# A graph layer on one TensorE: program order in the passes, and key fetches for two steps at once

## The chip, the cores and the metric

The kernel runs on one core of a Trainium2 chip. The metric is the device time of one execution in microseconds. The kernel before takes 17037.5 us, the median of three runs (17037.39 to 17084.01).

## What is computed

A node's features are normalised and cut off at zero. Every edge gives a message from its destination node and the difference of its source node to it, and each node adds the mean of its messages:

```python
h = jnp.maximum(_layernorm(x, axis=-1), 0.0)

local = h[dst]
nbr = h[src]
y = einsum('ec,oc->eo', concat([local, nbr - local]), W) + b
s = segment_sum(y, dst)
cnt = segment_sum(ones, dst)[:, None]
x = x + where(cnt > 0, s / maximum(cnt, 1.0), 0.0)
```

There are 100,000 nodes of 64 features and 3,300,000 edges, sorted by destination; the sources are random. Since the message is linear, what costs time is the sum, for each node, of the rows `h[src]`. The rows are held as three bf16 parts and a one, 193 columns (`CE`).

## The kernel before

The sum is computed in two ways that run side by side.

**Windows and passes.** The first 256 windows of 7936 edges are sorted by source (`sort_windows`, on VectorE (DVE) and ScalarE (ACT)) and the sorted keys written to `ksort` in DRAM. DVE then counts for each window where each block of source rows begins (line 596, `pos` at line 605) and makes a table `at` of addresses for the key fetches. A *cell* is one window's keys in 256 source rows; a *step* handles two cells (`i`), of 32 slots each, for the four windows (`QW`) of a set. `fill_slots` fetches the keys of a step, for all sets at once, by four indirect transfers of 128x32 keys (`kf`, line 716), issued by GpSimd (POOL), turns them into the numbers `srs` and `dts` and stores these. Keys beyond 32 in a cell are the *spill*: `find_beyond` fetches them by 128 indirect transfers of one key a row (`kx`, line 692), and DVE turns them into rows `xs` (line 698).

A pass keeps 40 blocks of `h` rows as tables (`tab`, line 759, fetched by SyncE (SP)) and goes through 64 sets of four windows, 40 steps each. In a step, `pick` multiplies one-hots `gh` (line 808) with the tables by 4 matmuls of 128x128 (line 829), ACT copies the result to `gs` (line 831), and `put` adds it by 16 quarter matmuls with one-hots `dh` (line 331 by `one_hot`, matmuls at line 838) into `total`. The loop goes by pairs of steps, with 8 matmuls of picks and 32 of puts each; picks run ahead of puts by two steps. After a set DVE reduces `total` to `wsums`. There are 5 passes: pass 0, in whose course the keys of later steps are fetched and the spill is found; passes 1 to 3 in a loop on the chip (line 957); pass 4 in two halves (line 959), in which sums are added to `acc` (line 880) and each set's spill is multiplied in (`rows_x`, line 794).

**Chunks.** The other 1,268,384 edges are 354 chunks of 128x28 edges (`chunks`). POOL gathers the rows of `h` by 28 indirect transfers a chunk (`nb`, line 388), DVE makes one-hots `hot` (line 331), TensorE (PE) sums them into `ps` by 28 matmuls (line 399), DVE reduces them to `sums` (lines 404 and 406), and POOL adds these to `acc` (line 357 by an indirect transfer, with addresses `to` from line 352, or line 362). There are six buffers of seven gathers for `nb`, so POOL may be 42 gathers ahead; the code of a matmul is emitted 21 gathers behind. 90 chunks belong to the sort stage and pass 0, 66 (`KB`) to each of passes 1 to 3, 33 to each half of pass 4. While windows are sorted and pass 0 runs, `gathers` interleaves them by estimated times (`GATHER` 1270 ns a gather); in `turn` they are spread evenly over the pairs of steps.

**Order.** The order of instructions on each engine is set by a scheduler, except where `last[engine]` ties one instruction behind another (`behind`, `tc.issue_after`). Nothing ties a chunk's matmuls or the picks and puts on PE, so the scheduler places them. Additions are put off: `add_later((LAG - 1) * J, ...)` (line 408) makes a chunk's addition due 56 gathers after its sums.

## Time and profile before

| what | value |
|---|---|
| median of three runs | 17037.5 us |
| the profiled execution | 17007.46 us |
| its span, from first to last instruction | 17005.8 us |
| TensorE matmuls busy | 12381.4 us (73% of the span) |
| DVE busy | 12270.0 us (72%) |
| POOL busy | 12313.7 us (72%) |
| ACT busy | 7284.1 us (43%) |
| 9912 gathers of chunks on POOL (line 388) | 10098.9 us busy, 3811.3 us idle ahead of them |

Busy shares are means over stages with different limits, so the table alone doesn't tell what bounds the kernel. A row of instructions by line has the line, the engine, the operation, what is written and read, the count, then busy time and mean nanoseconds of one, and the idle time of the engine just ahead with what ended it; "issue" there means that the engine waited for nothing that the profile shows. A row of waits has the waiting instruction, what released it, the sum in us, the count and the longest. A row of a line's instructions has the least, median and largest duration in ns, then the first begin and the last end in us.

### The profile page before, as it was taken

To read this page: it belongs to the slowest core of one execution; us is meant where nothing else is said; L and a number is where in the kernel's file an instruction comes from. 1 tells how busy PE (TensorE), PEld (TensorE's weight loads), DVE (VectorE), ACT (ScalarE), POOL (GpSimd) and SP (SyncE) were. 2 spreads that over 40 slices of the span, in tenths; PEclk is the share of its full clock that TensorE was granted. 3 is DMA by queue.
4 is the path that set the end of the run, shared out by engine and by line. 5 is a ranking of instruction groups with operands and counts; after the bars stand their busy time and mean duration, and the time that the engine had idled before them with its cause. 6 is when DMAs were issued, how large, how long until landed. Compare 5 with 4: busy or idle time off the path is not lost. (4 is left out here: it accounts for less than half of the span.)

```text
span 17005.8 us, 639895 instructions
## 1 busy us (share of the span) xinstructions
PE 12381.4 (73%) x266812; PEld 9784.7 (58%) x266812; DVE 12270.0 (72%) x31051; ACT 7284.1 (43%) x15555; POOL 12313.7 (72%) x11723
## 2 busy tenths in 40 slices
PE   6111111559999799999699999699999698858775
PEld 5011000447777577777577777477777576647664
DVE  6999982558878687777587777587777576647663
ACT  5244480335555344444354444254444343324331
POOL 4777777665675477777677777767777778767885
PEclk7555555779999899999799999799999798879887
DMA  7322222324454455555455555455555565556556
GB/s 293 70 39 40 49 49 58 86 73 115 120 121 120 112 128 123 124 124 122 112 127 123 124 124 123 110 128 124 122 124 123 112 125 112 113 100 121 112 111 250
DMA packets 1672971, 1949.85 MB, mean 115 GB/s; under 512 B 1065318, under 2 KB 1078766, under 8 KB 1665070
## 3 DMA queue, kind: packets, MB, share of 16 engines
q1 hardware_dynamic: 1194800, 1341.60, 27.4%
q0 software_dynamic: 471200, 541.36, 20.4%
q8 instruction: 2090, 34.24, 0.8%
q10 hardware_dynamic: 4032, 25.69, 0.4%
q14 instruction: 849, 6.96, 0.1%
HBM read 1652.22 MB, written 255.28 MB: 112 GB/s over the span
## 5 line engine op out<-in xcount | busy, mean ns | idle before, releaser
L388 POOL DMA_INDIRECT nb<-h,si x9912 | 10098.9, 1019 | 3811.3 <-issue 2714.6
L831 ACT CAST gs<-gp 128x386 bf16<-128x386 f32 x12800 | 5591.9, 485 | 7358.8 <-PE gp L829 6820.4
L331 DVE TENSOR_TENSOR dh<-dt,upto 128x512 bf16<-128x512 int16 x12800 | 4575.9, 419 | 1979.7 <-PE total L838 1697.2
L838 PE MATMUL total<-gs,dh 32*128 32x193 bf16 x200704 | 5542.2, 251 | 304.8 <-DVE dh L331 288.3
L829 PE MATMUL gp<-tab,gh 128*128 128x193 bf16 x50176 | 5509.6, 253 | 129.8 <-ACT gs L831 83.6
L838 PEld LDWEIGHTS <-dh 32*128 32x128 bf16 x200704 | 4125.9, 96 | 1490.7 <-issue 1099.5
L829 PEld LDWEIGHTS <-gh 128*128 128x128 bf16 x51200 | 4404.5, 100 | 1000.1 <-issue 861.6
L399 PE MATMUL ps<-nb,hot 128*128 128x193 bf16 x9912 | 2106.6, 278 | 3659.3 <-DMA nb<-h,si 2151.3
L808 DVE TENSOR_SCALAR gh<-srs,who_f 128x768 bf16<-128x768 int16 (+1 forms) x10240 | 3415.0, 393 | 643.5 <-PE gp L829 638.5
L399 PEld LDWEIGHTS <-hot 128*128 128x128 bf16 x9912 | 896.7, 105 | 4107.8 <-issue 2294.4
L331 DVE TENSOR_TENSOR hot<-near,upto 128x512 bf16<-128x512 int16 (+1 forms) x2832 | 925.6, 382 | 397.4 <-PE ps L399 393.0
L460 ACT COPY tmp<-keys 128x1536 f32<-128x1536 f32 (+26 forms) x525 | 647.7, 1244 | 1043.3 <-DVE keys L462 880.0
L716 POOL DMA_INDIRECT kf<-ksort,at x784 | 788.5, 1006 | 238.9 <-issue 228.9
L461 DVE TENSOR_TENSOR keys<-tmp,keys 128x1536 f32<-128x1536 f32 (+26 forms) x525 | 746.8, 1457 | 68.4 <-ACT tmp L460 67.2
L462 DVE TENSOR_TENSOR keys<-tmp,keys 128x1536 f32<-128x1536 f32 (+26 forms) x525 | 748.3, 1454 | 1.1
L868 DVE TENSOR_REDUCE wsums<-whole 128x512 f32<-128x1536 f32 x320 | 613.2, 1916 | 3.7 <-issue 2.1
L404 DVE TENSOR_REDUCE sums<-ps 128x64 f32<-128x192 f32 x354 | 123.6, 349 | 535.6 <-PE ps L399 532.4
L880 POOL DMA_DIRECT2D acc<-wsums x256 | 345.1, 1348 | 105.2 <-DMA acc<-wsums 91.0
L865 DVE COPY whole<-total 128x386 f32<-128x386 f32 x640 | 325.6, 550 | 52.2 <-ACT whole L863 52.2
L536 ACT ACTIVATE junk<-keys,bound 128x543 bf16<-128x543 f32 x450 | 337.4, 750 | 16.9 <-DVE keys L462 3.6
L863 ACT COPY whole<-total 128x386 f32<-128x386 f32 x640 | 276.4, 484 | 124.8 <-PE total L838 120.8
L362 POOL DMA_DIRECT2D acc<-sums x264 | 272.7, 1033 | 42.7 <-DMA acc<-wsums 17.4
(163 smaller groups left out, 4233.2 us busy)
## 6 DMA issues: line engine op xcount, KB each, us to landing
srs<-sr_d SPq DMA_DIRECT2D x2560, 320.0 KB
nb<-h,si POOLq DMA_INDIRECT x9912
part_d<-wsums SPq DMA_DIRECT2D x256, 260.0 KB
prev<-part_d SPq DMA_DIRECT2D x256, 260.0 KB
tab<-h SPq DMA_DIRECT2D x46, 970.0 KB
dt<-dt_d SPq DMA_DIRECT2D x2560, 10.0 KB
h<-parts SPq DMA_DIRECT2D x28, 1358.0 KB
dt_d<-dt SPq DMA_DIRECT2D x40, 640.0 KB
```

What stands on the lines that cost most here:

```text
L331: nc.vector.tensor_tensor(out.rearrange("p k (a d) -> p k a d", d=D), numbers[:, :, None].to_broadcast(shape), upto[:shape[0], :n].rearran ...
L388: last[POOL] = nc.gpsimd.indirect_dma_start(out=nbs[e // JN][:, e % JN], out_offset=None, in_=h3, in_offset=bass.IndirectOffsetOnAxis(ap=o ...
L399: nc.tensor.matmul(ps[:, :CE], lhsT=hots_of[d // JH][:, d % JH], rhs=nbs[d // JN][:, d % JN, :CE], start=jd == 0, stop=jd == J - 1)
L460: last[ACT] = nc.scalar.copy(tmp, lo)
L461: nc.vector.tensor_tensor(lo, tmp, hi, ALU.min)
L462: last[DVE] = nc.vector.tensor_tensor(hi, tmp, hi, ALU.max)
L716: last[POOL] = nc.gpsimd.indirect_dma_start(out=kf[:, c, r * KS:r * KS + KS], out_offset=None, in_=ksort, in_offset=bass.IndirectOffsetOnA ...
L808: nc.vector.tensor_scalar(ghots[v, k][:, part, a:z].rearrange("p c i s -> p (c i s)"), srs[v, k][:, a:z].rearrange("p c i s -> p (c i s)") ...
L829: nc.tensor.matmul(gp[:, i], lhsT=ghots[v, k][:, b, c, i], rhs=of[:, :CE], start=b == 0, stop=b == NT - 1)
L831: nc.scalar.copy(gs[t], gp)
L838: nc.tensor.matmul(total[:, r, b * CE:b * CE + CE], lhsT=dh[at, i, b * P:b * P + P], rhs=rows_of[at, i, :CE], start=begin and i == 0 and b ...
L868: nc.vector.tensor_reduce(sums[:, :, :C], whole[:, :, :C3].rearrange("p k (s c) -> p k c s", s=3), axis=AX.X, op=ALU.add)
```

## The change

1. `in_turn` ties the chunk matmuls, the first matmul of every pick and put and those of a set's own rows to the program's order on PE. `turn` starts that order afresh.
2. A chunk's addition is due 14 gathers (`JH`) after its sums instead of 56.
3. The four fetches of a step now fetch 95 keys from each address instead of 32 and serve two neighbouring cells (`kw`). The second cell's keys begin `far` behind the first; for every bit of `far` a `copy_predicated` on DVE moves the keys by that power of two. For this the two halves of a step become two contiguous ranges of source rows, so the tables are loaded by two transfers each. There are 392 such fetches and 4 plain ones instead of 784.
4. A window's spill may hold 32 keys instead of 64: 64 fetches `kx` of which four go out at a time, in order on POOL, and `xs` is computed four turns later, behind the latest `dh`. Each set has one `rows_x` fetch instead of two, and its matmuls are half as many.
5. `KB` is 64, so 98 chunks belong to the sort stage and pass 0.
6. A flag sends inputs with a cell of 64 or more keys, or more than 32 spilled keys in a window, down another way. In the inputs here the largest cell has 42 keys and a window has at most 17 spilled.

```diff
-KB = 66
+KB = 64
...
-SPILL = 2 * KS
+SPILL = KS
+NBITS = 6
+KW = KS + 2 ** NBITS - 1
...
+        def in_turn(ins):
+
+            if ins.ins.engine in last:
+                tc.add_manual_dep(ins.ins, last[ins.ins.engine].ins.name,
+                                  mybir.DependencyInfo(mybir.DependencyClass.NoSync, mybir.DependencyReason.DATA),
+                                  reason="in turn")
+            last[ins.ins.engine] = ins
...
-                    nc.tensor.matmul(ps[:, :CE], lhsT=hots_of[d // JH][:, d % JH], rhs=nbs[d // JN][:, d % JN, :CE],
-                                     start=jd == 0, stop=jd == J - 1)
+                    in_turn(nc.tensor.matmul(ps[:, :CE], lhsT=hots_of[d // JH][:, d % JH],
+                                             rhs=nbs[d // JN][:, d % JN, :CE], start=jd == 0, stop=jd == J - 1))
...
-                        add_later((LAG - 1) * J, lambda q=qd, t=to0[:, u0:u0 + 1], s=sums: addition(q, t, s))
+                        add_later(JH, lambda q=qd, t=to0[:, u0:u0 + 1], s=sums: addition(q, t, s))
...
-            kx = piece.tile([P, P], I32, name="kx", bufs=1)
-            for w in range(P):
-                last[POOL] = nc.gpsimd.indirect_dma_start(
+            kx = piece.tile([P, SETS], I32, name="kx", bufs=1)
+            for w in range(SETS):
+                in_turn(nc.gpsimd.indirect_dma_start(
                     out=kx[:, w:w + 1], out_offset=None, in_=ksort,
-                    in_offset=bass.IndirectOffsetOnAxis(ap=xat[:, w:w + 1], axis=0))
-                if w % 8 == 7:
+                    in_offset=bass.IndirectOffsetOnAxis(ap=xat[:, w:w + 1], axis=0)))
+                if w % 4 == 3:
                     yield
-            xs = piece.tile([P, P], I32, name="xs", bufs=1)
-            nc.vector.tensor_scalar(xs, kx, 10, None, op0=ALU.logical_shift_right)
+            for _ in range(4):
+                yield
+            xs = piece.tile([P, SETS], I32, name="xs", bufs=1)
+            with tc.issue_after(latest[0].ins):
+                nc.vector.tensor_scalar(xs, kx, 10, None, op0=ALU.logical_shift_right)
...
-                        for r in range(QW):
-                            last[POOL] = nc.gpsimd.indirect_dma_start(
-                                out=kf[:, c, r * KS:r * KS + KS], out_offset=None, in_=ksort,
-                                in_offset=bass.IndirectOffsetOnAxis(ap=at[:, r, s:s + 1], axis=0))
...
+                nc.vector.tensor_tensor(far[:, :, :n], at[:, :, s0 + 1:s0 + 2 * n:2], at[:, :, s0:s0 + 2 * n - 1:2], ALU.subtract)
...
+                    if q < n:
+                        kw = piece.tile([P, QW, KW], I32, name="kw", bufs=3)
+                        for r in range(QW):
+                            last[POOL] = nc.gpsimd.indirect_dma_start(
+                                out=kw[:, r], out_offset=None, in_=ksort,
+                                in_offset=bass.IndirectOffsetOnAxis(ap=at[:, r, s:s + 1], axis=0))
+                        nc.vector.tensor_copy(to[0].rearrange("p (r s) -> p r s", r=QW), kw[:, :, :KS])
+                        for i in reversed(range(NBITS)):
+                            m = KS + (1 << i) - 1
+                            nc.vector.copy_predicated(kw[:, :, :m], bits[:, i, :, q:q + 1].to_broadcast([P, QW, m]),
+                                                      kw[:, :, 1 << i:m + (1 << i)])
+                        nc.vector.tensor_copy(to[1].rearrange("p (r s) -> p r s", r=QW), kw[:, :, :KS])
...
-                tab = load.tile([P, SL * NB, CT], BF16, name=f"tab{k}", bufs=1)
-                nc.sync.dma_start(tab[:, :m * NB], h3[ds((g * SG + k * SL) * CS, m * CS)].rearrange("(x p) f -> p x f", p=P))
+                tab = load.tile([P, 2, SL * NT, CT], BF16, name=f"tab{k}", bufs=1)
+                for i in range(2):
+                    nc.sync.dma_start(tab[:, i, :m * NT],
+                                      h3[ds((i * NCB + g * SG + k * SL) * CELL, m * CELL)].rearrange("(x p) f -> p x f", p=P))
...
+                    latest[0] = one_hot(dhots[v, k][:, c], dts[v, k][:, c], CH)
...
+                        mm = nc.tensor.matmul(gp[:, i], lhsT=ghots[v, k][:, b, c, i], rhs=of[:, :CE],
+                                              start=b == 0, stop=b == NT - 1)
+                        if i == b == 0:
+                            in_turn(mm)
+                last[PE] = mm
...
+                            if i == b == r == 0:
+                                in_turn(mm)
+                last[PE] = mm
...
                 def turn(g, n, base, at, kb, final):
+                    last.pop(PE, None)
```

What the change moves stands in the order of each engine's instructions. First DVE before, directly after the last of the counting instructions (line 596), where the next `pos` (line 605) comes 35 rows further on:

```order
L596 TENSOR_SCALAR junk,pos<-keys 128x543
L331 TENSOR_TENSOR hot<-near,upto 128x384 x2
L404 TENSOR_REDUCE sums<-ps 128x64
L406 COPY sums<-ps 128x1
L331 TENSOR_TENSOR hot<-near,upto 128x512 x2
L331 TENSOR_TENSOR hot<-near,upto 128x384 x2
```

The same place of the changed kernel, in which the counting is line 607 and `pos` line 616:

```order
L607 TENSOR_SCALAR junk,pos<-keys 128x543
L342 TENSOR_TENSOR hot<-near,upto 128x384 x2
L360 TENSOR_SCALAR near<-rel 128x896
L358 TENSOR_TENSOR rel<-di,base_b 128x224
L616 TENSOR_SCALAR pos<-pos 128x392
L621 TENSOR_SCALAR edge<-pos 128x392
```

The one-hots and sums of chunks that stood between the counting and `pos` now stand behind the table of addresses. On POOL this is the place of the first key fetches before (`nb` are gathers, the `acc` rows additions), with 1806 gathers ahead of the first fetch:

```order
L357 DMA acc<-sums,to 100352x65
L388 DMA nb<-h_61,si 128x194 x21
L716 DMA kf<-ksort,at 128x32 x220
L388 DMA nb<-h_61,si 128x194 x7
L357 DMA acc<-sums,to 100352x65
```

And in the changed kernel, with 1589 gathers ahead:

```order
L368 DMA acc<-sums,to 100352x65
L399 DMA nb<-h_61,si 128x194
L765 DMA kw<-ksort,at 128x95 x112
L399 DMA nb<-h_61,si 128x194 x7
L765 DMA kw<-ksort,at 128x95 x20
L399 DMA nb<-h_61,si 128x194 x8
L368 DMA acc<-sums,to 100352x65
```

The fetches begin 217 gathers earlier in POOL's order and are half as many. On PE, this is the start of passes 1 to 3 before; the two rows of `hot` and `ps` go on alike until 96 chunk matmuls have been listed, and then the first pick follows:

```order
L957 COMPARE_AND_BRANCH
L957 UNCONDITIONAL_BRANCH x2
L1083 BRANCH_PREFETCH_HINT
L399 LDWEIGHTS hot
L399 MATMUL ps<-nb,hot 128x193
```

In the changed kernel pass 0 ends with 166 chunk matmuls in a row (the first two rows here are the last of them), and a later pass begins with picks (line 865); its first chunk matmul comes after 15 pairs of steps:

```order
L410 LDWEIGHTS hot
L410 MATMUL ps<-nb,hot 128x193
L1000 COMPARE_AND_BRANCH
L1000 UNCONDITIONAL_BRANCH x2
L1126 BRANCH_PREFETCH_HINT
L865 LDWEIGHTS gh
L865 MATMUL gp<-tab_82951,gh 128x193
```

So the chunk matmuls that stood at the start of a pass in a row are now spread over its pairs of steps, one or two to each, and in pass 0 1550 of 2744 stand ahead of the first pick, where it was 1806 of 2520.

More of the change, by code (lines that the diff above doesn't have):

```diff
@@ L26 @@
 ACT = mybir.EngineType.Activation
+PE = mybir.EngineType.PE
 P = 128
@@ L636, in sort_windows @@
                 nc.sync.dma_start(at[half].rearrange("g r c -> g (r c)"), at_d[i].rearrange("(g r) c -> g (r c)", r=QW))
-                nc.gpsimd.iota(first[half, :NCB], pattern=[[CS, NCB]], base=(BIAS >> 10) + i * CELL, channel_multiplier=0)
+                nc.gpsimd.iota(first[half, :NCB], pattern=[[CELL, NCB]], base=(BIAS >> 10) + i * NCB * CELL, channel_multiplier=0)
             nc.vector.memset(first[:, NCB:], (BIAS >> 10) + NCB * CS)
@@ L708, in fill_slots, with sources @@
             at, first = slots[:2]
-            for c0 in range(0, NS, SL):
-                kf = piece.tile([P, SL, P], I32, name="kf", bufs=2)
-                for c in range(SL):
-                    s = c0 + c
-                    if s < NCB:
-                        for r in range(QW):
-                            last[POOL] = nc.gpsimd.indirect_dma_start(
-                                out=kf[:, c, r * KS:r * KS + KS], out_offset=None, in_=ksort,
-                                in_offset=bass.IndirectOffsetOnAxis(ap=at[:, r, s:s + 1], axis=0))
-                    else:
-                        last[POOL] = nc.gpsimd.indirect_dma_start(
-                            out=kf[:, c], out_offset=None, in_=ksort,
-                            in_offset=bass.IndirectOffsetOnAxis(ap=at[:, s - NCB, NCB:], axis=0))
-                    if c == SL // 2:
-                        yield
+            def sources(c0, kf):
                 df = piece.tile([P, SL, P], F32, name="df", bufs=1)
@@ L747, in fill_slots @@
                 yield
+            kfs = {}
+            for s0 in range(0, NS, 2 * SL):
+                for k in range(2):
+                    kfs[s0 + k * SL] = piece.tile([P, SL, P], I32, name="kf", bufs=3)
+                n = min(SL, (NCB - s0) // 2)
+                far = piece.tile([P, QW, SL], I32, name="far", bufs=1)
+                nc.vector.tensor_tensor(far[:, :, :n], at[:, :, s0 + 1:s0 + 2 * n:2], at[:, :, s0:s0 + 2 * n - 1:2], ALU.subtract)
+                bits = piece.tile([P, NBITS, QW, SL], I32, name="bits", bufs=1)
+                for i in range(NBITS):
+                    nc.vector.tensor_scalar(bits[:, i, :, :n], far[:, :, :n], i, 1, op0=ALU.logical_shift_right, op1=ALU.bitwise_and)
+                for q in range(SL):
+                    s = s0 + 2 * q
+                    to = [kfs[t - t % SL][:, t % SL] for t in (s, s + 1)]
+                    if q < n:
[10 more added lines that the diff above has]
+                        nc.vector.tensor_copy(to[1].rearrange("p (r s) -> p r s", r=QW), kw[:, :, :KS])
+                    else:
+                        for t, k in zip((s, s + 1), to):
+                            last[POOL] = nc.gpsimd.indirect_dma_start(
+                                out=k, out_offset=None, in_=ksort,
+                                in_offset=bass.IndirectOffsetOnAxis(ap=at[:, t - NCB, NCB:], axis=0))
+                    if q % 2 == 0 and q < SL - 1:
+                        yield
+                for c0 in (s0, s0 + SL):
+                    yield from sources(c0, kfs.pop(c0))
         def passes(g, n, base, final):
@@ L792, in fetch @@
                     xs, xt, rows_x = beyond[v]
-                    for i in range(2):
-                        last[POOL] = nc.gpsimd.indirect_dma_start(
-                            out=rows_x[:, i], out_offset=None, in_=h3,
-                            in_offset=bass.IndirectOffsetOnAxis(ap=xs[:, i:i + 1], axis=0))
+                    last[POOL] = nc.gpsimd.indirect_dma_start(
+                        out=rows_x[:, 0], out_offset=None, in_=h3,
+                        in_offset=bass.IndirectOffsetOnAxis(ap=xs, axis=0))
             def one_hots(t, part):
@@ L837, in by_quarters @@
                             at = slice(r * KS, r * KS + KS)
-                            nc.tensor.matmul(total[:, r, b * CE:b * CE + CE], lhsT=dh[at, i, b * P:b * P + P],
-                                             rhs=rows_of[at, i, :CE], start=begin and i == 0 and b == 0, stop=stop,
-                                             skip_group_check=True)
+                            mm = nc.tensor.matmul(total[:, r, b * CE:b * CE + CE], lhsT=dh[at, i, b * P:b * P + P],
+                                                  rhs=rows_of[at, i, :CE], start=begin and i == 0 and b == 0, stop=stop,
+                                                  skip_group_check=True)
+                            if i == b == r == 0:
+                                in_turn(mm)
+                last[PE] = mm
             def put(t):
@@ L851, in put @@
                         for b in range(NT):
-                            nc.tensor.matmul(total[:, r, b * CE:b * CE + CE], lhsT=dh[:, i, b * P:b * P + P],
-                                             rhs=of[:, i], start=False, stop=False, skip_group_check=True)
+                            in_turn(nc.tensor.matmul(total[:, r, b * CE:b * CE + CE], lhsT=dh[:, i, b * P:b * P + P],
+                                                     rhs=of[:, i], start=False, stop=False, skip_group_check=True))
                 if s < SG - 1:
@@ L856, in put @@
                 if final:
-                    dx = hots.tile([P, 2, CH], BF16, name="dx", bufs=1)
+                    dx = hots.tile([P, 1, CH], BF16, name="dx", bufs=1)
                     one_hot(dx, beyond[v][1], CH)
```

53 lines of the change are left out of this document (25 added, 28 removed).

## The prediction

> **What bounds the kernel now.** The first view is the windows by stage: stretches of the span with the busy time of each engine, then the granted TensorE clock, the DMA share and GB/s. I cut it where the trace shows a stage begin: end of the sort's counting (2515), first key fetch (2855), first pick (3069), then pass ends.
>
> ```profile
> core 0: us, PE busy (x) PEld busy (x) DVE busy (x) ACT busy (x) POOL busy (x), PEclk, DMA share, GB/s
> 431.00:2515.00 2084.00, 313.31 (x1548) 203.78 (x1549) 1977.34 (x2410) 1019.98 (x1425) 1583.21 (x1603) 0.50 0.25 49
> 2515.00:2855.00 340.00, 82.16 (x256) 25.98 (x256) 46.66 (x154) 0.00 (x0) 259.25 (x266) 0.50 0.27 50
> 2855.00:3069.00 214.00, 12.02 (x47) 8.07 (x46) 87.27 (x283) 26.07 (x48) 163.41 (x167) 0.50 0.33 73
> 3069.00:5605.00 2536.00, 2134.74 (x52075) 1706.05 (x52073) 1853.99 (x5252) 1267.29 (x2881) 1561.77 (x1493) 0.93 0.43 107
> 5605.00:8226.00 2621.00, 2311.22 (x53048) 1835.52 (x53048) 1960.85 (x5608) 1165.91 (x2688) 1964.53 (x1914) 0.92 0.52 122
> 8226.00:10842.00 2616.00, 2307.28 (x53048) 1834.99 (x53048) 1962.03 (x5616) 1165.65 (x2688) 1956.92 (x1914) 0.92 0.52 122
> 10842.00:13457.00 2615.00, 2313.22 (x53048) 1837.39 (x53048) 1961.41 (x5615) 1165.98 (x2688) 1963.36 (x1914) 0.92 0.53 122
> 13457.00:15068.00 1611.00, 1224.92 (x25500) 966.75 (x25500) 1007.92 (x2841) 585.82 (x1344) 1224.18 (x1149) 0.85 0.58 111
> 15068.00:16677.00 1609.00, 1210.91 (x25500) 955.83 (x25500) 1007.05 (x2841) 584.61 (x1344) 1233.10 (x1149) 0.87 0.58 111
> 16677.00:17005.80 328.80, 199.27 (x1176) 180.79 (x1176) 137.40 (x227) 56.06 (x112) 200.74 (x56) 0.80 0.81 315
> 6200.00:8000.00 1800.00, 1647.20 (x37902) 1319.40 (x37901) 1405.54 (x4013) 834.08 (x1923) 1398.47 (x1366) 0.94 0.53 123
> ```
>
> The sort is DVE's (1977 of 2084 us). Between 2515 and 2855 DVE does 47 us of work and only POOL is busy. Pass 0 is nearest to PE. In passes 1 to 3 PE is busiest by busy time, but its clock leaves room, and in the steady stretch (last row) POOL issues 1366 instructions in 1800 us, 1.318 us each. What holds there is read from POOL's own lines and waits in pass 2:
>
> ```profile
> L388 POOL DMA_INDIRECT nb<-h,si x1848 | 1888.5, 1022 | 651.3 <-issue 502.4 <-PE ps L399 86.2 <-PE gp L829 26.2
> L362 POOL DMA_DIRECT2D acc<-sums x66 | 68.5, 1038 | 4.7 <-DMA acc<-sums 2.4 <-DVE sums L406 2.2
> POOL nb L388 <- PE ps L399: 86.2, 21, 23.4
> ```
>
> Each gather costs 1.02 us and an issue gap of 0.27 that nothing releases, so POOL alone makes 1914 x 1.318 = 2523 of the pass's 2616 us. The other 93 are 86 us in which gathers wait for the buffers that chunk matmuls free, and 7 at the ends. **Passes 1 to 3 are POOL's.** The chunk matmuls that free buffers come late because 96 of them stand on PE ahead of the first pick, and then none for a while:
>
> ```profile
> 8500.00:8550.00 50.00, 49.95 (x1268) 39.77 (x1257) 42.78 (x126) 27.85 (x65) 7.82 (x9) 1.00 0.43 110
> 8400.00:8550.00 150.00, 78.89 (x3004) 58.45 (x2992) 1.00 0.48 124
> ```
>
> The first row is POOL starved (9 instructions in 50 us) with PE full; the second is the puts alone (line 838): 3004 / 32 = 93.9 pairs of steps in 150 us, 1.598 us a pair when PE waits for nothing.
>
> **The change: the end of the sort.** These are instructions by line with begin and end, and POOL's lines in the sort stage.
>
> ```profile
> L596 DVE TENSOR_SCALAR_CACHE_REDUCE junk<-keys x334: 703/719/721, 2189.9 to 2513.8; 128x543 bf16<-128x543 f32 x167
> L605 DVE TENSOR_SCALAR pos<-pos x2: 184/366/548, 2689.7 to 2818.6; 128x392 f32<-128x392 f32 x1, 128x58 f32<-128x58 f32 x1
> L716 POOL DMA_INDIRECT kf<-ksort,at x784: 940/947/2992, 2854.9 to 5386.9; - x196
> L388 POOL DMA_INDIRECT nb<-h,si x1550 | 1496.3, 965 | 496.0 <-issue 440.7 <-PE ps L399 25.3 <-DMA nb<-h,si 13.7
> L357 POOL DMA_INDIRECT acc<-sums,to x53 | 87.3, 1646 | 16.1 <-issue 11.0 <-DVE keys L461 1.8 <-DVE keys L462 1.5
> ```
>
> Counting ends at 2514, but the positions (`pos`) come only at 2690 and 2818, behind one-hots and sums of chunks whose gathers POOL delivers at (1496.3 + 496.0) / 1550 = 1.285 us. Afterwards `pos` stands directly behind the counting, with one chunk one-hot and its preparation between. The remaining DVE and transfer steps took 2818 to 2855, so `at` is ready by about 2515 + 8 (my allowance for those few and `pos`) + 37 = 2560. POOL has 39 more gathers ahead of its first key fetch (1589 against the 1550 done): 39 x 1.285 + 2 additions x 1.95 = 54, about 2570. First key fetch 2855 to **2570: -285**.
>
> **Fetches for two steps.** Here are POOL's lines from 2855 to 5605, and the sort's `copy_predicated`, the only ones of that operation.
>
> ```profile
> L716 POOL DMA_INDIRECT kf<-ksort,at x784 | 788.5, 1006 | 238.9 <-issue 228.9 <-DMA kf<-ksort,at 6.1 <-ACT gs L831 4.0
> L388 POOL DMA_INDIRECT nb<-h,si x714 | 762.3, 1068 | 538.1 <-PE ps L399 329.6 <-issue 193.2 <-PE gp L829 9.1
> L357 POOL DMA_INDIRECT acc<-sums,to x29 | 49.5, 1707 | 43.3 <-DVE sums L406 35.0 <-issue 4.9 <-DVE dh L331 1.5
> L452 DVE COPY_PREDICATED s<-own,q x16: 1010/1293/1294, 468.0 to 572.0; 128x1024 int32<-128x1024 int32 x14, 128x768 int32<-128x768 int32 x2
> ```
>
> A fetch is (788.5 + 238.9) / 784 = 1.31 us on POOL. Ahead of the first pick now stand 112 wide ones, 147 us. A fetch of 95 keys for 32 isn't shown; the gathers of 194 numbers (965 to 1068 ns) say that POOL's part doesn't grow. So the first pick moves from 3069 to 2570 + 147 + 8 (again an allowance, for the last keys' way to a one-hot) = **2725: -344** so far. On DVE each pair of steps gains six `copy_predicated` over 996 elements in all and two copies. By the row, 1293 ns for 1024 elements and 1010 for 768 make 1.105 ns an element and 161 ns fixed: 996 x 1.105 + 6 x 161 = 2.07 us, some 2.6 with two copies, is the upper end, and 1.4, if an element costs half of that and the copies nothing more than 0.1, the lower: 102 to 190 us over the 73 pairs that fall into pass 0 (25 come before it), most of it beside PE's work.
>
> **Pass 0 (steps on PE).** The waits around its beginning, then puts (line 838) and chunk matmuls (line 399) in its steady part, then four neighbouring rows of the timeline:
>
> ```profile
> PE total L838 <- DVE dh L331: 250.1, 2, 166.0
> DVE xs L698 <- DMA kx<-ksort,xat: 169.1, 1, 169.1
> DVE to L352 <- DMA acc<-sums,to: 88.7, 1, 88.7
> 3710.00:5440.00 1730.00, 831.11 (x31008) 612.48 (x31008) 0.98 0.49 120
> 3710.00:5440.00 1730.00, 95.90 (x619) 55.72 (x619) 0.98 0.49 120
> 5413.06 0.85 PE L838 MATMUL total<-gs,dh 32*128 32x193 bf16 x32
> 5414.64 0.85 PE L838 MATMUL total<-gs,dh 32*128 32x193 bf16 x32
> 5415.42 0.26 PE L399 MATMUL ps<-nb,hot 128*128 128x193 bf16 x1
> 5416.29 0.85 PE L838 MATMUL total<-gs,dh 32*128 32x193 bf16 x32
> ```
>
> The 128 spill fetches held DVE for 169 us and PE for 166 behind it; DVE also stood 89 us at `to`. Afterwards the spill fetches go out in fours, their use comes four yields later, and additions are due early: both stalls go. The rate is 1730 / 969 = 1.785 us a pair, with 0.64 chunk matmuls. One chunk matmul between puts takes the gap from 1.58 (5413.06 to 5414.64) to 1.65, so 0.08 with rounding. PE then needs 1280 pairs x 1.598 = 2045, plus what the steady rate has beyond that, (1.785 - 1.598 - 0.05) x 1280 = 172, plus 1028 chunk matmuls x 0.08 = 82: 2299. Between nothing and DVE's added 190 us I take 70 for places where PE waits for it: 2370, to 5095. Behind the last put stand 166 chunk matmuls; POOL is some 38 gathers ahead, so 128 x 1.285 + 5 additions x 2 + 12 = 187. Pass 0 ends at **5282 instead of 5605: -323**. POOL's work from 2570 (396 fetches x 1.31, 64 spill fetches x 1.25, 1155 gathers x 1.34, 41 additions x 1.87 = 2221) ends at 4791 at the earliest, so it isn't the limit.
>
> **Passes 1 to 3.** 64 x 28 = 1792 gathers and 64 additions: 1856 x 1.318 = 2446, the 86 us gone, 9 at the ends, and 25 for a start at which picks wait for the tables (tables come in 16 transfers, 8 more; between 0 and 30 us). That is **2480 for 2616: -137 each, -412**. PE's busy time of 2307 goes down by 56 matmuls, so PE fits, with 140 us to spare.
>
> **The two halves.** POOL's lines of 13457 to 15068:
>
> ```profile
> L388 POOL DMA_INDIRECT nb<-h,si x924 | 954.3, 1033 | 291.3 <-issue 256.3 <-PE gp L829 10.3 <-DMA di<-in_dst_p 8.5
> L880 POOL DMA_DIRECT2D acc<-wsums x128 | 172.0, 1343 | 52.5 <-DMA acc<-wsums 43.4 <-DMA acc<-sums 4.6 <-DMA own<-h 3.5
> L794 POOL DMA_INDIRECT rows_x<-h,xs x64 | 65.2, 1019 | 23.8 <-issue 18.8 <-DMA xs<-xs_d 4.6 <-DMA nb<-h,si 0.3
> ```
>
> POOL again: 1245.6 + 224.5 + 89 + 33 additions (49) = 1608. Afterwards 896 x 1.34 = 1201, 224.5, half of 89, 32 additions (48), 10 at the ends, 25 at the start: **1552: -58 each, -116**.
>
> **At nothing:** additions due after 14 gathers (0 to 0.5 us each on POOL, with up to 42 gathers queued ahead to cover it), three buffers of fetched keys, 8 fewer spill matmuls a set, first and last stage. The sum: -323 - 412 - 116 = -851, span 16155 for 17006. The profiled execution took 17007.5, the median 17037.5, 30 above: **16190**.
>
> **Rivals.** (B) PE becomes the bound. A late gather now holds every pick behind it, and a wait costs clock:
>
> ```profile
> 7012.38 0.32 PE L399 MATMUL ps<-nb,hot 128*128 128x193 bf16 x1 [0.96 <-DMA nb<-h,si]
> 7012.49 1.50 PE L829 MATMUL gp<-tab,gh 128*128 128x193 bf16 x8
> ```
>
> Eight picks take 1.50 us there, against 0.85 for the warm groups above. If PE holds 2306 busy and idles 8% between, a pass is about 2550: +70 each, +30 in pass 0, **16430**. Against it: 0.94 in the steady part although such waits stand in it. (C) DVE bounds pass 0: 1854 + 190 busy and a dependence at every step gives 2570: +200, **16390**. (D) Slower: in program order each chunk matmul's wait comes round, and the clock stays low through all passes, as at 0.50 in the sort stage where PE has only single chunk matmuls. Busy time of 2307 at 0.92 is 2122 / clock: at 0.80, 2652 + 85 a pass, +257 three times, and pass 0 +373: **17310**. It decides at about 0.82, where the loss eats the 851. Against it: the halves, with PE idle 24% of the time, still have 0.85. (E) Nothing is lost between DVE and PE in pass 0 (-70), nor at three pass starts (-75), and the chunk tail of pass 0 is a quarter shorter (-45): **16000**. That the change doesn't do what it says would need the way back for large cells: cells have at most 42 keys and windows at most 17 spilled, under 64 and 32.
>
> A rule that bears on D: the Trainium skill, page "TensorE: Matmul & The Clock Gate", section "A second HAM failure mode: psum-queue depth-cycling", says that many short idle times between groups of matmuls let the clock swing between half and full. The slowed group at 7012 agrees for one group; 0.94 over 1800 us doesn't for the stage. By that rule alone the sum would come out near D.
>
> **How the numbers follow.** Forecast 60%, B 15%, C 12%, E 8%, D 5%. Range: 16190 less 70, 75 and 1.8 us per hundred gathers (1.300 instead of 1.318, 33 a pass) is 15950; B with tables at 30 us four times is 16550. Only D lies outside, with some of the tails. A measurement of this kernel tells 0.3% (51 us) from no change: faster 0.93, same 0.02, slower 0.05.
>
> **What would show it.** Right: first key fetch near 2570, first pick near 2725, no `kx` wait of 100 us, pass 0 ending near 5280 with some 190 us of chunk matmuls alone, passes of 2480 with POOL at 1.32 us an instruction and no long `PE ps` wait, clock 0.9 or more. Wrong: POOL waiting for PE throughout the passes (B), PE waiting for `gh` or `dh` from DVE in pass 0 (C), a clock near 0.8 (D).

## The result and the profile after

The changed kernel takes 16326.6 us (median of 4 runs, 16308.1 to 16339.38) where the kernel before takes 17040.52: the ratio is 0.9575, with a 95% interval of 0.9555 to 0.9594. The forecast was 16190, in a range of 15950 to 16550. The profiled execution has a span of 16306.4 us, 151 more than the 16155 of the sum.

This is the view of windows by stage for the changed kernel, cut at the same events as before: end of the counting, first key fetch, first pick, last put of pass 0, then the ends of the chunk tail, of passes 1 to 3 and of the two halves. The columns are those of the table in the prediction.

```profile
2515.00:2569.00 54.00, 0.69 (x2) 0.08 (x1) 20.57 (x70) 0.00 (x0) 41.52 (x41) 0.50 0.50 104
2569.00:2707.00 138.00, 10.63 (x40) 7.42 (x40) 82.53 (x331) 26.87 (x49) 106.15 (x105) 0.50 0.49 132
2707.00:5073.00 2366.00, 2165.64 (x52325) 1709.17 (x52325) 2045.28 (x6110) 1263.36 (x2876) 1528.16 (x1416) 0.99 0.46 123
5073.00:5254.00 181.00, 46.40 (x233) 17.56 (x231) 17.18 (x54) 1.62 (x4) 136.58 (x140) 0.52 0.42 91
5254.00:7740.00 2486.00, 2221.02 (x52992) 1772.84 (x52992) 1953.06 (x5590) 1160.87 (x2688) 1931.44 (x1856) 0.98 0.49 123
7740.00:10251.00 2511.00, 2211.13 (x52992) 1765.77 (x52992) 1955.05 (x5600) 1159.68 (x2688) 1929.70 (x1856) 0.97 0.50 126
10251.00:12751.00 2500.00, 2212.23 (x52992) 1766.36 (x52992) 1951.87 (x5584) 1159.78 (x2688) 1931.47 (x1856) 0.98 0.50 126
12751.00:14365.00 1614.00, 1194.97 (x25216) 953.46 (x25216) 996.01 (x2828) 587.01 (x1344) 1145.91 (x1088) 0.88 0.51 109
14365.00:15978.00 1613.00, 1201.19 (x25216) 957.89 (x25216) 995.68 (x2828) 587.71 (x1344) 1147.35 (x1088) 0.88 0.51 109
```

Stage by stage, against the forecast:

| stage | before, us | forecast | after | after less forecast |
|---|---|---|---|---|
| first key fetch at | 2855 | 2570 | 2569 | -1 |
| first pick at | 3069 | 2725 | 2707 | -18 |
| steps of pass 0 | 2536 | 2370 | 2366 | -4 |
| chunk tail behind them | none | 187 | 181 | -6 |
| passes 1, 2, 3 | 2621, 2616, 2615 | 2480 each | 2486, 2511, 2500 | +57 in all |
| the halves of pass 4 | 1611, 1609 | 1552 each | 1614, 1613 | +123 in all |
| last stage | 329 | 329 | 328 | -1 |

The first pick's -18 contains the -1 of the first fetch; the other rows add up to the 151 us. Two of them outweigh the rest: the halves gained nothing (+123), and the passes a little less than forecast (+57). The halves' reason stands in POOL's lines of the first half and in its longest wait there:

```profile
L399 POOL DMA_INDIRECT nb<-h,si x896 | 916.0, 1022 | 285.6 <-issue 249.3 <-DMA nb<-h,si 11.6 <-PE gp L865 7.9
L922 POOL DMA_DIRECT2D acc<-wsums x128 | 166.2, 1298 | 161.9 <-DMA acc<-wsums 152.5 <-issue 7.1 <-DVE sums L417 2.2
L373 POOL DMA_DIRECT2D acc<-sums x32 | 32.7, 1023 | 2.4 <-DMA acc<-wsums 2.4
POOL acc L922 <- DMA acc<-wsums: 152.5, 63, 5.3
```

The gathers cost the 1201.6 us that the sum has for them, but the 128 additions of sets' sums (`wsums`) cost 166.2 + 161.9 = 328 instead of 224.5. Against these 104 us too much stand some 13 less for the chunks' additions (35.1 for 48) and some 32 less at the start and the ends (3 for 35), so that a half misses by 62. Most of their idle time is one thing: an addition waits until the one ahead has landed, 63 times, 2.4 us each. The timeline of POOL shows how they stand (start, duration, and in brackets the idle time ahead):

```profile
13431.21 1.37 POOL L922 DMA_DIRECT2D acc<-wsums  x1
13434.83 1.22 POOL L922 DMA_DIRECT2D acc<-wsums  x1 [2.25 <-DMA acc<-wsums]
13436.35 1.23 POOL L399 DMA_INDIRECT nb<-h,si  x1 [0.30 <-issue]
13439.30 1.24 POOL L922 DMA_DIRECT2D acc<-wsums  x1 [1.72 <-DMA acc<-wsums]
```

Two of this set's four additions stand side by side, and the third is one gather behind. An addition reads and writes `acc`, and the program makes the next one wait until it has landed; here that was 3.6 us after its start. In the first half of the kernel before, four instructions or more stand between any two additions in 26 of the 32 sets. In that of the changed kernel the first two are neighbours in all 32; in 19 sets the third comes one instruction behind them, in 12 directly behind, in one all four stand together.

The other parts of the forecast are seen in these rows of the changed kernel: `pos` straight behind the counting, the first fetch, PE's waits for DVE in pass 0 (2707 to 5073), POOL's waits for chunk matmuls in that stretch, and the gathers in pass 1.

```profile
L616 DVE TENSOR_SCALAR pos<-pos x2: 183/270/358, 2516.5 to 2520.1; 128x392 f32<-128x392 f32 x1, 128x58 f32<-128x58 f32 x1
L765 POOL DMA_INDIRECT kw<-ksort,at x392: 938/954/4086, 2569.0 to 4647.2; - x196
PE total L877 <- DVE whole L907: 64.7, 36, 16.8
PE gp L865 <- DVE gh L844: 47.2, 54, 20.4
PE total L877 <- DVE dh L342: 14.2, 16, 3.3
POOL nb L399 <- PE ps L410: 309.8, 60, 13.2
L399 POOL DMA_INDIRECT nb<-h,si x1792 | 1865.7, 1041 | 545.9 <-issue 475.2 <-PE gp L865 32.6 <-DMA nb<-h,si 26.5
```

PE has no wait of 100 us left in pass 0, and POOL waits 310 us for PE in pass 0, so pass 0 is PE's as forecast. In pass 1 a gather takes 1041 ns where it took 1022.

### The profile page after: what moved, and what is told of

Its sections match the earlier page's. It is cut to its first block, busy times and chain, and to the rows that moved or that the text cites. A ratio compares the mean times of both kernels' runs of the same rounds, so it can differ in the third digit from the quotient of the medians.

```text
span 16306.4 us, 639004 instructions
## 1 busy us (share of the span) xinstructions
PE 12051.6 (74%) x266300; PEld 9566.6 (59%) x266300; DVE 12400.5 (76%) x31837; ACT 7270.1 (45%) x15555; POOL 11887.4 (73%) x11203
## 3 DMA queue, kind: packets, MB, share of 16 engines
q8 instruction: 2086, 34.18, 0.8%
## 5 line engine op out<-in xcount | busy, mean ns | idle before, releaser
L877 PE MATMUL total<-gs,dh 32*128 32x193 bf16 x200704 | 5465.0, 247 | 408.0 <-DVE whole L907 377.6
L865 PE MATMUL gp<-tab,gh 128*128 128x193 bf16 x50176 | 5419.6, 250 | 349.3 <-DVE gh L844 227.6
L865 PEld LDWEIGHTS <-gh 128*128 128x128 bf16 x51200 | 4487.9, 99 | 1410.2 <-issue 967.4
L877 PEld LDWEIGHTS <-dh 32*128 32x128 bf16 x200704 | 3997.4, 94 | 1479.3 <-issue 926.8
L410 PE MATMUL ps<-nb,hot 128*128 128x193 bf16 x9912 | 2231.0, 274 | 3012.8 <-DMA nb<-h,si 1519.6
L410 PEld LDWEIGHTS <-hot 128*128 128x128 bf16 x9912 | 862.6, 103 | 3281.0 <-issue 1654.0
L765 POOL DMA_INDIRECT kw<-ksort,at x392 | 427.3, 1090 | 211.4 <-issue 94.5
```

The lines of the kernel that those rows point to most:

```text
L410: in_turn(nc.tensor.matmul(ps[:, :CE], lhsT=hots_of[d // JH][:, d % JH], rhs=nbs[d // JN][:, d % JN, :CE], start=jd == 0, stop=jd == J - 1))
L765: last[POOL] = nc.gpsimd.indirect_dma_start(out=kw[:, r], out_offset=None, in_=ksort, in_offset=bass.IndirectOffsetOnAxis(ap=at[:, r, s:s ...
L865: mm = nc.tensor.matmul(gp[:, i], lhsT=ghots[v, k][:, b, c, i], rhs=of[:, :CE], start=b == 0, stop=b == NT - 1)
L877: mm = nc.tensor.matmul(total[:, r, b * CE:b * CE + CE], lhsT=dh[at, i, b * P:b * P + P], rhs=rows_of[at, i, :CE], start=begin and i == 0 ...
```

## The experiments

Each run is compared with the kernel before on its own chip. On two chips (the first five runs here) the kernel before itself takes 25554 and 25951 us; these are told apart from the others, at the end of this section. On the chips of the other seven it takes 16994 to 17016 us.

**Control, and the fetch for two steps undone.** The control is the changed kernel itself. In the other run the branch with `kw` is replaced:

```diff
-                        kw = piece.tile([P, QW, KW], I32, name="kw", bufs=3)
...
+                        for t, k in zip((s, s + 1), to):
+                            for r in range(QW):
+                                last[POOL] = nc.gpsimd.indirect_dma_start(
+                                    out=k[:, r * KS:r * KS + KS], out_offset=None, in_=ksort,
+                                    in_offset=bass.IndirectOffsetOnAxis(ap=at[:, r, t:t + 1], axis=0))
```

> The changed kernel unaltered, as the control for the runs beside it. Theory: on a chip that takes 17040 us for the kernel before it takes 16330; where PE's instructions come late (the kernel before at 25500 to 26000 us), the time follows PE's 532000 instructions and not POOL's, so the change is worth about as much as its edits to the beginning, 700 to 1300 us of 25554, and the late wsums additions, which touch POOL alone, nothing measurable beside it. Rival: late wsums additions are worth their 200 us there too.

> The changed kernel with key fetches of one step each again, 784 of 32 keys, and without the copy_predicated and copies; all else kept. Theory: the first pick comes (224 - 112) x 1.31 = 147 us later, less what DVE waited for there, so near 2840 instead of 2707; in pass 0 POOL has 280 fetches more (367 us), which stays under PE's 2366, and DVE 130 us less to do, so pass 0's steps take 2300 to 2370: about +100 us in all (16430 for 16330). Rival: POOL becomes the bound of pass 0 without the fetch for two steps, the steps take over 2550 us and the whole 16600 or more; or DVE's copies cost what the fetches saved and the time doesn't move by 50 us.

The control took 16275.36 us beside 17003.6 for the kernel before, a ratio of 0.957 again. With single fetches it took 16513.32: 238 us more than the control, not 100 (one run each). These are its windows from the first fetch to the first pick and from there to the last put of pass 0, and PE's waits for DVE in the second stretch; the last row is a wait of DVE itself, for a load of stored numbers:

```profile
2569.00:2780.00 211.00, 10.64 (x41) 7.55 (x42) 53.49 (x234) 25.72 (x48) 160.41 (x167) 0.50 0.33 74
2780.00:5320.00 2540.00, 2157.66 (x52325) 1716.20 (x52324) 1898.27 (x5358) 1261.76 (x2878) 1811.39 (x1746) 0.95 0.46 113
...
PE total L871 <- DVE whole L901: 122.6, 37, 63.4
PE gp L859 <- DVE gh L838: 114.2, 8, 54.9
PE total L871 <- DVE dh L342: 37.3, 3, 23.3
...
DVE dh L342 <- DMA dt<-dt_d: 91.7, 2, 63.8
```

The first pick comes only 73 us later, but the steps of pass 0 take 2540 us instead of 2366. PE's busy time is about the same (2158 us for 2166); what is added are waits for DVE, single ones of up to 63 us. Since DVE does less here than with double fetches (1898 us instead of 2045), it isn't full but held up itself. In this stretch it waits 158 us in five waits for loads of the numbers that are made of fetched keys (`dt` 91.7, `srs` 65.9), and 89 us in three for chunk additions ahead of `to`; in the control these are 24 and 6 us. The last key fetch goes out at 5017 instead of 4651, and POOL's instructions with their issue gaps come to some 2290 of the 2540 us. So the keys come late, and POOL has less room than expected; what delayed each load was not followed further. The fetch for two steps is worth 238 us, most of it inside pass 0, and the time lies between the expectation and its rival (steps over 2550 us).

**The order on PE: taken away, and alone.** The first run has `in_turn` do nothing for PE; the second is the kernel before with `in_turn` on its chunk matmuls, picks and puts, and nothing else of the change.

```diff
         def in_turn(ins):
 
+            if ins.ins.engine == PE:
+                return
```

> The changed kernel without the program's order on PE, all else kept. Theory: the order on PE is what brings the key fetches forward: first fetch at about 2850 us instead of 2569 (+281); passes 1 to 3 some 2540 to 2570 us (+150 in all), since chunk matmuls are hoisted again; the 64 spill fetches stand in one block but little waits for them: about 16750 us. Rival: PE's order costs as much in waits within the passes as it brings, the passes stay at 2500 without it and the time is near 16600.

> The kernel before with nothing but the program's order on PE. Theory: first fetch near 2570 instead of 2855 (-285), passes 1 to 3 at 1914 x 1.318 + 40 = 2563 instead of 2616 (-160 in all), the halves unchanged near 1610, pass 0 shortened by the start at full rate but still with a wait of some 165 us behind the spill fetches and all fetches of one step: about 16500 us. Rival: pass 0 becomes POOL's, since 784 fetches and the chunk gathers that now stand behind the first pick add up, and gives back 150 us or more of the 285: 16700.

Without the order it took 16918.2 us; the order alone took 16564.75, beside 17015.93. First three rows of the run without the order (`pos`, the first fetches, and the window from the last put of pass 0 to the end of pass 3), then three of the run with the order alone (its fetches, the window of passes 1 to 3, and DVE's wait behind the spill fetches):

```profile
L618 DVE TENSOR_SCALAR pos<-pos x2: 185/368/550, 2690.5 to 2820.8; 128x392 f32<-128x392 f32 x1, 128x58 f32<-128x58 f32 x1
L767 POOL DMA_INDIRECT kw<-ksort,at x392: 939/953/3025, 2856.1 to 4957.8; - x196
5386.00:13212.00 7826.00, 6867.85 (x159208) 5438.25 (x159207) 5868.89 (x16828) 3495.75 (x8068) 5872.89 (x5707) 0.92 0.51 122
```

```profile
L725 POOL DMA_INDIRECT kf<-ksort,at x784: 940/949/3178, 2571.0 to 5122.0; - x196
5342.00:13074.00 7732.00, 6710.78 (x159148) 5352.97 (x159144) 5892.74 (x16849) 3479.81 (x8066) 5952.26 (x5742) 0.97 0.52 124
DVE xs L707 <- DMA kx<-ksort,xat: 174.2, 1, 174.2
```

Without the order on PE `pos` is back at 2690 and 2820 and the first fetch at 2856; with nothing but the order the first fetch is at 2571. So it is the order on PE, which ties chunk matmuls to their place and with them the sums behind them on DVE, that brings the 285 us at the end of the sort. In passes 1 to 3 the order alone saves 39 us a pass (7732 / 3 = 2577 for 2616), and its clock is 0.97 against 0.92 without it. With the order alone the wait behind the spill fetches stands as before, 174 us, and the steps of pass 0 (2784 to 5340, 2556 us) are not shorter than before (2536). The run with the order alone lies 65 us above its expectation. The run without the order lies 170 us above its own: its passes take 2609 us each (7826 / 3) and not 2540 to 2570, and its halves 1688 to 1690, where additions wait 350 us in the two together for the one ahead to land and PE's clock is 0.83. Each of the two is a single run.

**The additions of a set.** Two ways to take them apart: make `wsums` additions due later, or undo edit 2, so that a chunk's addition stands in the queue of additions for 56 gathers again.

```diff
-                    add_later(JH, addition)
+                    add_later(JH + LAGJ, addition)
```

```diff
-                        add_later(JH, lambda q=qd, t=to0[:, u0:u0 + 1], s=sums: addition(q, t, s))
+                        add_later((LAG - 1) * J, lambda q=qd, t=to0[:, u0:u0 + 1], s=sums: addition(q, t, s))
```

> The changed kernel with a set's sums (wsums) added 35 gathers after they are made instead of 14, on a chip on which the changed kernel takes some 16300 us. Theory: the 305 us for which these additions waited for the one ahead fall to some 30 to 90, each half of pass 4 takes about 1510 us instead of 1614, and the whole about 16100. Rival: the waits go to other instructions of POOL (gathers, rows_x) and the halves stay at 1600 us, 16300 in all.

> The changed kernel with a chunk's addition due 56 gathers after its sums again (edit 2 undone), on a chip on which the kernel before takes about 17010 us. Theory: edit 2 made the set's additions stand side by side, because the chunk's addition, due late, had stood ahead of them in the queue of additions; with it undone the halves take about 1500 us as with late wsums additions (1497), and the rest doesn't move: 16050 to 16080. Rival: the early additions were worth something elsewhere (the first key fetch, the wait at `to`, the buffers of sums in passes 1 to 3); then the first fetch comes after 2575 us or passes 1 to 3 take over 2520 us each, and the time is 16150 or more.

With late `wsums` additions: 16051.38 us, ratio 0.9431 (0.9415 to 0.9447). With edit 2 undone: 16153.48 us, ratio 0.9500 (0.9485 to 0.9516). The first pair of rows is of the run with late additions (the additions in its first half, and that half's window), the second group of the run with edit 2 undone (passes 1 to 3, both halves, and the wait of `wsums` additions in the whole run):

```profile
L922 POOL DMA_DIRECT2D acc<-wsums x128 | 175.2, 1369 | 16.2 <-DMA acc<-wsums 10.8 <-issue 2.9 <-DMA acc<-sums 2.1
12737.00:14234.00 1497.00, 1161.49 (x25216) 929.61 (x25216) 1007.93 (x2828) 584.99 (x1344) 1169.70 (x1088) 0.92 0.58 117
```

```profile
5282.00:12793.00 7511.00, 6636.15 (x158970) 5298.55 (x158968) 5846.10 (x16748) 3479.09 (x8064) 5802.09 (x5561) 0.98 0.52 125
12793.00:15832.00 3039.00, 2310.31 (x50432) 1848.69 (x50432) 2012.04 (x5656) 1168.30 (x2688) 2366.01 (x2176) 0.92 0.57 116
POOL acc L922 <- DMA acc<-wsums: 38.8, 18, 2.9
```

With four gathers between them in 30 of the 32 sets, the 128 additions idle 16 us instead of 162, and a half takes 1497 us instead of 1614; the whole lies some 50 us below its expectation. Undoing edit 2 takes the neighbours apart as well (39 us of wait in the whole run against 306), so edit 2 had caused them. Against the changed kernel's own windows the run with edit 2 undone has halves 188 us shorter (3039 for 3227), and they begin 42 us later (12793 for 12751). So edit 2 costs about 190 us in the halves and gives back some 40 ahead of them; by the ratios, 0.9500 for 0.9575, undoing it is a gain.

But the run with edit 2 undone came to its rival's time, 102 us slower than the one with late additions, although neither place that the rival names shows it (first fetch at 2571, passes of 2504 us each). From the windows: 24 us at the end of pass 0 (5282 for 5258), 32 in passes 1 to 3 (7511 for 7479), 45 in the halves (3039 for 2994). A group's end adds what is still in the queue, and there is more of it when additions are due late: pass 0 ends with three neighbouring additions, some 4 us apart, instead of two. But POOL's rows give this little of the 102: 7 us of waits for additions in the passes and 22 in the halves. Gathers that take longer account for 28 us in the passes (1044 ns for 1038) and 28 in the halves (1053 for 1038). The two runs were on different chips, so the cause of the 102 us stays open.

**A version meant to beat both.** Late `wsums` additions, `KB = 62`, and more gathers to a pair of steps in pass 0, so that no tail is left:

```diff
-KB = 64
+KB = 62
...
-STEP = 900
+STEP = 1095
```

> A version meant to beat both: the changed kernel with late wsums additions, 62 chunks to each later group instead of 64 (106 chunks in the sort stage and pass 0), and the estimated time of a step raised from 900 to 1095 ns, so that 1.11 gathers go with each pair of steps in pass 0 instead of 0.80 and no chunk matmul is left behind its last put. Theory: the tail of 181 us after pass 0 goes, pass 0's steps get 390 chunk matmuls more (about 30 us of PE) and POOL's work there comes to 2420 us, so they take some 2430 instead of 2366; passes 1 to 3 lose 58 POOL instructions of 1.318 us each (-76 each), the halves 104 of waits and 28 gathers (-140 each): about 15700 us. Rival: POOL becomes the bound of pass 0 with waits of PE on top, pass 0 takes over 2600 us and the whole 15880 or more.

It took 15830.35 us (15791.76 to 15861.97), ratio 0.9294 (0.9279 to 0.9310): faster than both kernels, but 130 above its expectation and close to its rival. These are the windows of pass 0's steps, passes 1 to 3 and the halves, and POOL's gathers in pass 0:

```profile
2707.00:5321.00 2614.00, 2222.20 (x52780) 1757.70 (x52780) 2087.94 (x6253) 1265.27 (x2877) 1936.82 (x1788) 0.95 0.48 118
5330.00:12614.00 7284.00, 6566.08 (x158808) 5260.00 (x158808) 5845.54 (x16708) 3476.97 (x8064) 5621.84 (x5394) 0.98 0.53 129
12614.00:15531.00 2917.00, 2299.35 (x50376) 1840.21 (x50376) 2012.40 (x5636) 1166.82 (x2688) 2280.31 (x2118) 0.92 0.59 119
...
L399 POOL DMA_INDIRECT nb<-h,si x1379 | 1462.3, 1060 | 471.6 <-issue 371.0 <-PE ps L410 55.0 <-PE gp L865 20.9
```

The tail is gone, passes and halves come out as expected (2428 and 1459 us each), but pass 0 takes 2614 us and not 2430. A gather costs POOL (1462.3 + 471.6) / 1379 = 1.40 us there with its waits. POOL's instructions and issue gaps come to some 2406 of the 2614 us, and PE, busy for 2222, waits 314 us for DVE. So POOL's work no longer fits beside PE's, as the rival has it, but no engine fills the stage by itself. Against the run with late additions passes 1 to 3 begin 72 us later (5330 for 5258), and they and the halves are shorter by 7479 + 2994 - 7284 - 2917 = 272 us.

**Chips on which PE pauses.** The first five runs, four of the kernels above and one of them twice:

> One edit to the changed kernel: a set's four sums (wsums) are added 35 gathers after they are made instead of 14, which puts four gathers between each two of these additions on POOL, where two stood side by side. Theory: in each half of pass 4 the 152 us for which wsums additions waited for the addition ahead of them to land come from those two neighbours. The wait falls to some 45 us, a half takes about 1510 us instead of 1614, and the whole about 16120. Rival: additions into acc land no faster than that whatever stands between them; the wait stays near 150 us and the time at 16330.

> One edit to the changed kernel: a chunk's addition is due 56 gathers after its sums again, as before the change. In the queue of additions the chunk's then stands ahead of the set's and spreads those out. Theory: the halves take about 1510 us as in the run with late wsums additions, and nothing else moves, so about 16120: the earlier addition of chunks bought nothing, and cost 200 us by the bunching. Rival: early additions are worth something in the sort stage or in the passes (buffers and the wait on `to`), in which case the first key fetch comes after 2569 or passes 1 to 3 take over 2520 us, and the time lies above 16180.

> The changed kernel without the program's order on PE (all else kept, POOL's order of spill fetches too). Theory: it is the order on PE that brings the key fetches forward and ends the hoisting of chunk matmuls. First key fetch back at about 2850 us, spill fetches in one block and again some 85 us of wait behind them, passes 1 to 3 about 2540 to 2570 us each: about 16850 us. Rival: the order on PE matters only for the passes, and the fetch for two steps or the early additions bring the rest; the first fetch stays near 2570 and the time is about 16500.

> The kernel before with nothing but the program's order on PE. Theory: first key fetch near 2570 instead of 2855 (-285), passes 1 to 3 about 1914 x 1.318 + 35 = 2558 instead of 2616 (-175 in all), the halves unchanged near 1610, the wait behind the spill fetches kept at some 165 us: about 16510. Rival: without the fetch for two steps and the short spill the gain at the end of the sort is lost again in pass 0, whose end stays within 100 us of 5605: about 16750.

> The kernel with late wsums additions once more, on a chip on which the kernel before takes its 17040 us (in the runs so far it took 25554, with idle time on PE that nothing releases). Theory: the wait of wsums additions for the one ahead falls from 152 us a half to some 45, a half takes 1510 us instead of 1614, the whole 16120. Rival: the wait stays near 150 us a half and the time at 16330.

Beside 25553.8 us for the kernel before: late additions 24124.85 (ratio 0.9441, 0.9425 to 0.9456), edit 2 undone 24675.38 (0.9655), no order on PE 24369.93, the order alone 25795.26. On the second chip, beside 25950.76, late additions took 24593.74. None of the times expected applies, since another thing bounds the kernel there. From the lines of the run with late additions, and from the timeline of its repetition:

```profile
L877 PE MATMUL total<-gs,dh 32*128 32x193 bf16 x200704 | 8080.2, 274 | 4444.6 <-issue 4162.0 <-DVE whole L907 247.2 <-ACT gs L870 10.1
```

```profile
12032.02 0.26 PE L877 MATMUL total<-gs,dh 32*128 32x193 bf16 x4
12032.59 0.35 PE L877 MATMUL total<-gs,dh 32*128 32x193 bf16 x6 [0.31 <-issue]
12033.35 0.32 PE L877 MATMUL total<-gs,dh 32*128 32x193 bf16 x5 [0.41 <-issue]
...
12035.56 0.48 PE L877 MATMUL total<-gs,dh 32*128 32x193 bf16 x5 [1.11 <-issue]
```

Inside one put, whose matmuls wait for nothing between them, PE stops here after every two to six for 0.3 to 1.1 us. In the whole run puts have 4162 us of idle time that nothing releases; in the run of 16051 us the same kernel has next to none (368 us idle ahead of puts, all but 1 of them in waits that something ends). The matmuls of puts take longer too, 274 ns in the mean for 246. What makes PE pause was not found. These runs are used only for what they show of order: the wait of `wsums` additions was 25 to 35 us with late additions or with edit 2 undone, and 303 without the order on PE, much as on the other chips (25, 39 and 350).

## Why the prediction came out as it did

**The end of the sort** was right in its size (2569 for 2570), and the two runs on PE's order show the cause: with the order alone the fetch is at 2571, without it at 2856. The prediction had read this from the order of rows and had not said which edit makes it.

**The fetch for two steps** was right in what it gave (first pick 2707 for 2725), but its main worth was missed. The prediction saw 147 us ahead of the first pick and no use inside pass 0, since POOL has room there. Undone, the first pick is 73 us later and pass 0's steps 174 us longer, in waits of PE for DVE, which itself waits for numbers made of fetched keys and for additions.

**Pass 0** came out at 2366 us for 2370, as PE's, with the stall behind the spill fetches gone. The order alone keeps this stall (174 us), and it is gone in each run that undoes the order, the early additions or the double fetches alone, which leaves the spill's edits. The terms of the 2370 fit less well than their sum, and that the sum came so near is in part luck: PE is busy 2166 us, less than the 2299, and idle 200, of which 126 are waits for DVE where the sum has 70. Of rival C, DVE's work came as it said (2045 us for 1854 + 190); the time did not.

**Passes 1 to 3** are POOL's, as said: 1931.4 us busy and 548.2 idle make 2480 of pass 1's 2486 us. The mechanism held. The term "1856 x 1.318" (2446) holds only with a gather at 1022 ns; it took 1041, which is 34 us for 1792 of them. In pass 1 this is made up by a start without the 25 us that the sum has there, so its 2486 for 2480 is in part luck. In pass 2 POOL does wait 31 us (18.1 for chunk matmuls, 12.6 for a load of numbers). Why a gather takes longer stays open.

**Rivals B and D.** B needed PE's busy time to stay at 2306 us with new waits on top, D needed its clock to fall. The clock rose, from 0.92 to 0.97 or 0.98 in the passes, and the busy time went down to between 2211 and 2221 us. These are PE's waits for gathers in pass 2, before and after:

```profile
PE ps L399 <- DMA nb<-h,si: 298.1, 268, 20.3
```

```profile
PE ps L410 <- DMA nb<-h,si: 155.3, 193, 2.7
```

The waits that the order was to bring round at every chunk matmul came at 193 of 1792, 0.8 us each. Before, 97 of the 268 waits, with the longest, stood in the pass's first 134 us (8226 to 8360), where the hoisted matmuls stood and the clock was 0.50. In the rest of the pass 171 waits (187 us, none over 4.1) left it at 0.99 up to 8700 and at 0.93 to 0.94 from there. So past the start number and length are much the same as after the change; what differs is that 103 of the 171 came in rows of three or more with starts less than 2.5 us apart, and after it only 33 of 193. That the rows cost the clock fits this, but no run tried it alone. The rule weighed for D, in the Trainium skill's page "TensorE: Matmul & The Clock Gate", section "A second HAM failure mode: psum-queue depth-cycling", has short idle times between groups of matmuls swing the clock; the single ones here left it at 0.97 in pass 2.

**The halves** are the step that failed. The prediction wrote "Afterwards 896 x 1.34 = 1201, 224.5, half of 89, 32 additions (48), 10 at the ends, 25 at the start: 1552", and put the earlier additions "at nothing". It carried over the 224.5 us of the `wsums` additions, whose line the change doesn't touch. But edit 2 changes the queue that they share with chunk additions, and with it their places on POOL: 328 us in the first half. Taking the neighbours apart makes the half 117 us shorter (1614 to 1497). How the earlier due time makes neighbours was not shown: in the program's order `add_now` lets an addition out only when four gathers (`GAP`) have gone since the last, in both kernels, so it is the scheduler that moves them together. Making either kind of addition due later ends it, which fits sums that were not ready at their place. The rows that show this were in the order of the changed kernel, on the engine that bounds the halves, and were not read there. The other terms of a half were 45 us too large together, which hid part of the miss.

**Slips that decide nothing.** The lower end for the copies is 1.6 us by its own figures, not 1.4 (118 us over 73 pairs, not 102). D's time by its terms is 17334, not 17310. A pass of 2480 leaves PE 173 us beside 2307, not 140. By its row a gather of the halves before costs 1.348 us and not 1.34, 7 us over 896; it came at 1201.6 / 896 = 1.341. And the 0.85 us set beside B's eight picks is that of puts, though eight picks at full clock take 0.85 as well (at 5413.85).

## What to carry to other kernels

When an edit changes when something leaves a shared queue, look at what else leaves that queue, and read the new order on the bounding engine for it, also where its own lines are untouched. In the stages that POOL's issue bounds, the sum of instruction times came within 31 us for passes of some 2500; in the halves, where read-modify-writes of one tensor became neighbours, it missed by 62 of 1614. Ties to program order on one engine can pay most on another: here PE's order brought DVE's address table forward by 285 us.

## What the runs showed of the hardware

Of two neighbouring additions into `acc` the second started 3.6 us after the first, held until that had landed; with four gathers between them (4 x 1.3 us) the wait was all but gone, 11 us for 128. PE's granted clock stood at 0.97 in a pass in which gathers held PE 193 times for 0.8 us each, mostly once between groups; before, past the first 134 us of the pass, 171 such waits, more than half of them in rows, left it at 0.93 to 0.94 for most of the time. And on two of the chips the same program ran half as long again (25554 and 25951 us for 17040); in the runs traced there, PE paused inside groups of ready matmuls. The Trainium skill, page "Runtime: NRT & Kernel Launch", section "Instruction fetch mechanics", says that each engine's instructions are streamed in by DMA in blocks while it executes, mostly hidden; pauses that nothing releases would fit a stream that falls behind, but no run here shows when its blocks arrive. The profile's instruction queue has 2086 packets of 34.18 MB in both runs with late additions, and their time is 0.6% of the DMA engines' span on the slower chip and 0.9% on the other, which is about the same time for spans of 24109 and 16059 us.
